# Linear-attention stage of a two-layer network: gate made by halves of an image, bias row added by GpSimd, first tokens turned later

## The chip, the cores and the metric

The kernel runs on one core of a Trainium2 chip, in fp32. The metric is the device time of one execution in microseconds (us), as the median of three runs: 2871.56 us before the change (2869.07 to 2872.76).

## What is computed

The input is 4 images of 32 x 32 pixels (1024 tokens) with 384 channels. Layer 0 is a deformable attention with convolved offsets; layer 1 is a linear attention and then a mixture of four experts of which each token takes two. Cut to what matters here:

```python
x = x + L0_conv(_gn(x), ...)          # ends in  out @ w_out + b_out
t = tokens(x)                          # 4 x 1024 tokens x 384
# layer 1, attention (12 heads of 32 channels)
q, k, v = split(_ln_t(t) @ qkv_w + qkv_b)
A = einsum('bhdn,bhne->bhde', f(k), f(v)) * gauss      # f(t) = t + 1 if t >= 0 else exp(t)
out = einsum('bhnd,bhde->bhne', q * d**-0.5, A - lam * A)
t = t + (out @ proj_w + proj_b)
# layer 1, experts
probs = softmax(_ln_t(t) @ gate_w + gate_b)            # 4 experts
masked = probs of the two largest, divided by their sum
h = gelu(_ln_t(t) @ w1[e] + b1[e]);  y = h @ w2[e] + b2[e]
t = t + sum over e of masked[e] * y[e]
```

`_ln_t` is a layer norm over the 384 channels.

## The kernel before

Tokens stand in tiles of 128 partitions by 384 channels, eight tiles an image. A token tile that goes into a matmul as the stationary or moving side has to be turned first (channels on partitions), by three 128x128 transposes on TensorE (PE) into PSUM and a copy to SBUF.[...]

**Layer 0 and its end (the first seam).** The work is cut into 24 units (image and head), each in `KP` = 4 steps, `NP` = 96 steps in all. A loop `for g in range(NP + 7)` (L1500 to L1559) issues the stages of a software pipeline by hand: in a manual schedule each engine gets its instructions in the order in which they are written. The last scores are done some steps before the last of these, so the last `g` hold only the tail of the pipeline: `values` (L1317, the product `po` of exponentiated scores S with v), `out_of` (L1348, ACT's copy `av`), `to_queries` (L1362, the turn `pr`, the reciprocal `ri` and the product `at`), `to_channels` (L1397, the turn `pi` and ACT's copy `ao`). When an image's six heads are through, `waiting` gets eight token tiles, and `project` (L1417) makes for each: load the input tile `xk` from memory, three matmuls `y`, GpSimd adds the bias row (L1438), DVE adds `y` (L1441), and the result is stored to `x1_d`. The tag `xk` has three places (bufs=3), which project's tiles rotate through. For the last image, the `while waiting` loop behind the main loop does these eight, with PSUM from three tags in turn.

In this tail the first layer norm of the linear stage is hidden: image 0's tokens, x0, have been loaded by `load_early`, and at `g == NP + 3` (L1549) all eight tiles are normalised by `layer_norm` (L1095: statistics of eight tiles, one inverse root, then tile by tile) into the tag `xk`, turned by PE (`c_tr`, L1555) and copied by ACT to `xT0`. In PE's written order these 24 transposes stand ahead of the last `po` product. The line `wqT` (L1725), nine transposes of a weight, is PE's first work of the linear stage.

**The linear stage.** It has no manual schedule; the order on each engine is that in which generators are stepped (L2020 to L2031):

```python
for part in (ahead, behind, behind):
    left = next(part, part) is not part or left
```

`ahead` is `keys(b + 1)` (L1907) and `behind` is `outputs(b)` (L1963), so the steps of two images alternate. `keys` normalises and turns the image's eight tiles, then makes for each tile keys and values (`c_kv`: six matmuls into two PSUM tiles), DVE's bias addition, the feature map (`ex`, Exp on ACT, then `fm` on DVE), and one tile later the product `pa`, 3 x 128 x 128; at its end `am` is `pa` times a constant mask. `outputs` folds `am` with the projection (`c_pg`, `c_g`), with the query weight (`c_pw`, `c_wx`) and the query bias (`c_pb`; with the projection's bias it is the row `rb`), each link waiting for the one before. Then come eight products `c_y` = turned tokens times `wx`. For each, DVE adds `rb` out of PSUM (`c_ysb`, L2011) and adds the sum to the token tile in xb (L2012). There is a step after every two tiles. PSUM: the tag `mm` has four banks, `tr` two, `ph` two.

At its end `outputs` steps through `gate(b)` (L1732): it stores the image's tokens to `out`, takes the layer norm's statistics of all eight tiles and one inverse root (`rstd_of`, L220: Sqrt on ACT and six small operations on DVE), then for each half of the image four times normalise (`tn`, L1747), turn (`d_tr`) and copy (`d_tT`), six matmuls `pl` for the logits, and a store of `tn` to memory (tn_d), where the experts gather tokens from. `tn` has one place, so the second half's first write waits for the first half's store. Then softmax and choice of two (small operations on DVE), the counts' products `pg` (L1810), the slots, 16 scatters of table entries by GpSimd (L1842), and the table of blocks. GpSimd takes its instructions in order, too: after image 0's round the call `fetch(0)` (L1659) puts a load of block 0's entries on SP's queue and a conversion and four gathers on GpSimd's.

**The experts (second seam).** 25 blocks of 512, 256 or 128 gathered tokens follow, each turned (`e_tr`), multiplied by w1 (`ph`, L2053) and w2 (`acc`, L2085). Block 0 needs image 0 only, but its turns stand in PE's order behind all of image 3's gate; with no image left to alternate with, nothing lies beside that gate.

Of the kernel before, what the change touches and what calls it, by code (L numbers as in the profile page):

```python
# [11 lines left out]
F32 = mybir.dt.float32  # L12
I32 = mybir.dt.int32
AF = mybir.ActivationFunctionType
ALU = mybir.AluOpType
# [4 lines left out]
P = 128  # L20
# [139 lines left out]
def body(  # L160
# [954 lines left out]
    with tc.tile_pool(name="b_w", bufs=1) as bwp, tc.tile_pool(name="b_qkv", bufs=2) as bq, tc.tile_pool(  # L1115
# [361 lines left out]

        with tc.manual_schedule(
# [22 lines left out]
            for g in range(NP + 7):  # L1501
# [47 lines left out]
                if g == NP + 3:  # L1549

                    for k, t in layer_norm(by, bm, x0, 0, "c_ln", tag="xk"):
                        if k % 4 == 0:
                            pt = bps.tile([P, 4, 512], F32, tag="s", name=f"c_tr0_{k}")
                        for c in range(CK):
                            nc.tensor.transpose(  # L1555
                                pt[:, k % 4, c * P : (c + 1) * P], t[:, c * P : (c + 1) * P], ident
                            )
                        nc.scalar.copy(
                            xT0[:, :, k * P : (k + 1) * P],  # L1559
                            pt[:, k % 4, :NC].rearrange("p (c j) -> p c j", c=CK),  # L1560
                        )
# [3 lines left out]
            while waiting:  # L1565
# [3 lines left out]
                for i in range(n):  # L1569
                    project(0, py[:, i, :])  # L1570
                    project(1)
                    project(2)

# [143 lines left out]
    with tc.tile_pool(name="c_1", bufs=1) as c1, tc.tile_pool(name="c_2", bufs=2) as c2, tc.tile_pool(  # L1717
# [14 lines left out]
        def gate(b):  # L1732

            nc.sync.dma_start(out_t[b].rearrange("(k p) c -> p k c", p=P), xb[b])
            mv = cs.tile([P, NB, 2], F32, tag="mv", name=f"d_lnmv{b}")
            for k in range(NB):
                st = cs.tile([P, 6], F32, tag="bn", name=f"d_lnbn{b}_{k}")
                nc.vector.bn_stats(st, xb[b][:, k, :])
                nc.vector.bn_aggr(mv[:, k, :], st)
            r = rstd_of(cs, mv[:, :, 1], 1e-5, [P, NB], f"d_lnr{b}")  # L1740

            pl = lmm.tile([P, 512], F32, tag="mm", name=f"pl{b}")
            for f in range(2):
                tT = c2.tile([P, CK, 512], F32, tag="tT", bufs=1, name=f"d_tT{b}_{f}")
                tn = c2.tile([P, 4, NC], F32, tag="tn", bufs=1, name=f"tn{b}_{f}")
                for k in range(4 * f, 4 * f + 4):
                    nc.vector.tensor_scalar(  # L1747
                        tn[:, k % 4, :], xb[b][:, k, :], mv[:, k, 0:1], r[:, k : k + 1], ALU.subtract, ALU.mult
# [158 lines left out]
        def keys(b):  # L1907
# [52 lines left out]
            am = c2.tile([P, CK, P], F32, tag="am", name=f"am{b}")  # L1960
# [4 lines left out]
        def outputs(b):  # L1965
# [31 lines left out]
            rb = c2.tile([P, NC], F32, tag="rb", name=f"c_rb{b}")  # L1997
            nc.vector.tensor_tensor(rb, ps[:, :NC], bproj, ALU.add)
            yield
# [206 lines left out]
```

## Time and profile before

| view | value |
|---|---|
| median of three runs | 2871.56 us |
| the profiled execution, its time beside its span | 2916.14 us, span 2914.4 us |
| PE busy, share of the span | 2620.1 us, 90% |
| DVE | 1589.4 us, 55% |
| ACT | 1149.0 us, 39% |
| GpSimd (POOL) | 817.4 us, 28% |
| mean granted PE clock | 0.959 |
| layer 0, to 1430 us: PE busy | 1199.1 of 1430.0 us |
| first seam, 1430 to 1480 us: PE busy | 36.1 of 50.0 us |
| linear stage to the first expert product, 1480 to 1814.6 us: PE busy | 303.2 of 334.6 us |
| experts, 1814.6 us to the end: PE busy | 1081.7 of 1099.8 us |
| DVE's two additions per y tile (L2011, L2012) | 32 x 0.543 and 32 x 0.558 us |
| GpSimd's addition of a row to a token tile (L1438) | 0.995 us |
| GpSimd's scatter of table entries (L1842) | 64 x 0.961 us |

The profile is of one execution, and all its times are from the start of its span. It is longer than the runs without a profiler, so sums made with its durations are compared with its own 2916.14 us first. A line such as L1555 is a line of the kernel. An instruction's idle time is that of its engine just before it, and the arrow names what ended that idle time; an engine named there as "remote" or "issue" is none that the profile could tell. A group or instruction that stands as "x3" in an order of time is three records that followed each other.

### The profile page before, as it was taken

To read this page: it belongs to the slowest core of one execution; us is meant where nothing else is said; L and a number is where in the kernel's file an instruction comes from. 1 tells how busy PE (TensorE), PEld (TensorE's weight loads), DVE (VectorE), ACT (ScalarE), POOL (GpSimd) and SP (SyncE) were. 2 spreads that over 40 slices of the span, in tenths; PEclk is the share of its full clock that TensorE was granted. 3 is DMA by queue.
4 is the path that set the end of the run, shared out by engine and by line. 5 is a ranking of instruction groups with operands and counts; after the bars stand their busy time and mean duration, and the time that the engine had idled before them with its cause. 6 is when DMAs were issued, how large, how long until landed. Compare 5 with 4: busy or idle time off the path is not lost. (4 is left out here: it accounts for less than half of the span.)

```text
span 2914.4 us, 33271 instructions
## 1 busy us (share of the span) xinstructions
PE 2620.1 (90%) x12731; PEld 1295.6 (44%) x12731; DVE 1589.4 (55%) x2357; ACT 1149.0 (39%) x1522; POOL 817.4 (28%) x744
## 2 busy tenths in 40 slices
PE   8679957888898988889799997999999999999999
PEld 5345522333333333233256554555555555555566
DVE  3668867999999999999647665101001101011011
ACT  4354526777767667666422221111111111111111
POOL 1528873232333323233000223322111112121121
PEclk9789977999999999999899998999999999999999
DMA  7824475554555655454121311543222334474271
GB/s 198 238 66 134 129 220 169 154 150 141 153 160 174 187 154 155 139 156 139 28 100 44 123 44 55 182 152 124 101 100 101 105 136 144 150 249 168 100 268 64
DMA packets 267899, 404.77 MB, mean 139 GB/s; under 512 B 134674, under 2 KB 207634, under 8 KB 267356
## 3 DMA queue, kind: packets, MB, share of 16 engines
q1 hardware_dynamic: 214912, 230.43, 25.1%
q0 software_dynamic: 52112, 172.15, 18.6%
q8 instruction: 100, 1.64, 0.2%
q14 instruction: 59, 0.48, 0.1%
q10 hardware_dynamic: 716, 0.07, 0.0%
HBM read 345.68 MB, written 70.06 MB: 143 GB/s over the span
## 5 line engine op out<-in xcount | busy, mean ns | idle before, releaser
L2053 PE MATMUL ph<-d_xT,w 128*128 128x512 f32 (+1 forms) x1152 | 483.9, 554 | 1.2 <-ACT h L2060 1.2
L2085 PE MATMUL acc<-w,h 128*128 128x384 f32 x1392 | 480.3, 486 | 0.0
L1221 PE MATMUL ps<-q,k 64*64 64x512 f32 x1536 | 384.0, 614 | 93.3 <-DVE S L1252 46.5
L1168 POOL DMA_INDIRECT win<-table,widx x192 | 279.7, 1457 | 643.0 <-DVE t L1194 611.7
L2060 ACT ACTIVATE h<-ph,b1c 128x512 f32<-128x512 f32 (+1 forms) x192 | 124.1, 647 | 776.3 <-PE ph L2053 711.5
L1226 PE MATMUL ps<-o,ident 64*64 64x512 f32 x1536 | 380.4, 615 | 8.4 <-ACT o L1202 8.4
L2085 PEld LDWEIGHTS acc<-w,h 128*128 128x128 f32 x1392 | 264.1, 190 | 208.5 <-issue 73.2
L2053 PEld LDWEIGHTS ph<-d_xT,w 128*128 128x128 f32 x1152 | 216.8, 191 | 196.2 <-issue 144.3
L871 POOL DMA_INDIRECT ga<-img,pidx x192 | 230.3, 1199 | 187.7 <-DVE w L828 65.7
L2115 POOL DMA_INDIRECT out<-rows,ei x67 | 67.2, 1002 | 700.0 <-DVE rows L2112 691.2
L1221 PEld LDWEIGHTS ps<-q,k 64*64 64x64 f32 x1536 | 99.2, 135 | 358.6 <-issue 215.4
L1315 ACT ACTIVATE S<-S 128x2048 f32<-128x2048 f32 x96 | 183.4, 1911 | 190.1 <-DVE S L1311 190.1
L1252 DVE SCALAR_TENSOR_TENSOR S<-t,bw,ps 128x1024 f32<-128x1024 f32 x192 | 236.9, 1275 | 21.0 <-PE ps L1226 18.0
L1194 DVE SCALAR_TENSOR_TENSOR t<-win,bw,t 128x1056 f32<-128x1056 f32 x192 | 244.5, 1314 | 5.2 <-ACT t L1184 4.0
L1709 DVE COPY d_xT<-e_tr 128x512 f32<-128x512 f32 (+2 forms) x75 | 36.5, 511 | 372.7 <-PE e_tr L1706 372.7
L2104 DVE SCALAR_TENSOR_TENSOR rows<-b2r,en,rows 128x384 f32<-128x384 f32 x67 | 40.8, 618 | 364.2 <-DMA rows<-out,ei 258.2
L1184 ACT ACTIVATE t<-win,bw 128x1056 f32<-128x1056 f32 x192 | 218.1, 1168 | 37.7 <-DMA win<-table,widx 36.4
L1202 ACT ACTIVATE o<-t,bw 128x1024 f32<-128x1024 f32 x192 | 212.8, 1144 | 37.2 <-DVE t L1194 29.2
L1311 DVE TENSOR_TENSOR S<-S,pbs 128x2048 f32<-128x2048 f32 x96 | 218.9, 2282 | 2.0 <-ACT pbs L1306 2.0
L1329 PE MATMUL po<-S,v 128*64 128x512 f32 x768 | 197.7, 638 | 23.8 <-ACT av L1354 13.6
L2112 DVE SCALAR_TENSOR_TENSOR rows<-acc,en,rows 128x384 f32<-128x384 f32 x67 | 41.4, 618 | 219.1 <-PE acc L2085 217.6
L713 PE MATMUL pcv<-qpad,wc 64*64 64x256 f32 x1728 | 121.4, 396 | 27.3 <-issue 26.6
(350 smaller groups left out, 3442.6 us busy)
## 6 DMA issues: line engine op xcount, KB each, us to landing
w<-in_L_ffn_w SPq DMA_DIRECT2D x50, 2304.0 KB
img<-in_x SPq DMA_DIRECT2D x48, 256.0 KB
q<-q_d SPq DMA_DIRECT2D x48, 256.0 KB
x<-in_x SPq DMA_DIRECT2D x8, 768.0 KB
q_d<-qt SPq DMA_DIRECT2D x24, 256.0 KB
v_d<-qkvw SPq DMA_DIRECT2D x32, 192.0 KB
v<-v_d SPq DMA_DIRECT2D x24, 256.0 KB
k<-k_d SPq DMA_DIRECT2D x48, 128.0 KB
```

Of the source, the lines that this page charges most:

```text
L871: nc.gpsimd.indirect_dma_start(out=ga[:, g].rearrange("p s c -> p (s c)"), out_offset=None, in_=img[b][:, :], in_offset=bass.IndirectOffse ...
L1168: nc.gpsimd.indirect_dma_start(out=win, out_offset=None, in_=tables[h // 2][:, :], in_offset=bass.IndirectOffsetOnAxis(ap=widx[b][:, nb, h ...
L1184: nc.scalar.activation(t.rearrange("p y x -> p (y x)"), wins[p, e][:, : HI * WIN], AF.Copy, scale=weight(p, e, 0),)
L1194: nc.vector.scalar_tensor_tensor(tf, wins.pop((p, e))[:, WIN:], weight(p, e, 1), tf, ALU.mult, ALU.add)
L1202: nc.scalar.activation(o, ts[p, e][:, :, 0:WI], AF.Copy, scale=weight(p, e, 2))
L1221: made.append(nc.tensor.matmul(ps[HALF[1 - r], e, FULL[f]], k[HALF[r], 2 * kp + e, :], q[HALF[r], FULL[f]], start=(step == 0), stop=(step ...
L1226: made.append(nc.tensor.matmul(ps[HALF[r], d, FULL[f]], ident[HALF[r], HALF[r]], os_[p, d][HALF[r], FULL[f]], start=(step == 0), stop=(ste ...
L1252: nc.vector.scalar_tensor_tensor(st[:, e, :].rearrange("p (y x) -> p y x", x=WI), ts.pop((p, e))[:, :, 1:WIN], weight(p, e, 3), ps[:, e, : ...
L1311: nc.vector.tensor_tensor(Ss[p], Ss[p], bc(pbss[p // KP][:, :], 1, 2), ALU.add)
L1329: nc.tensor.matmul(pos[i][0][HALF[f], :], vs[i][:, 2 * kp + e, :], Ss[p][:, e, FULL[f]], start=(first and e == 0), stop=(last and e == 1),)
L2053: nc.tensor.matmul(ph if short(d) else ph[:, :n], a, m, start=(c == 0), stop=(c == CK - 1))
L2085: nc.tensor.matmul(d["acc"][0 if short(d) else s][:, :NC], h[:, s * P : (s + 1) * P], d["w2"][:, hc, :], start=(hc == 0), stop=(hc == HC - 1),
```

## The change

- **First tokens turned later.** `layer_norm` of image 0 becomes a generator that the loop steps. At `g == NP + 3` it makes the statistics and the first normalised tile. `turn_first(n)` turns the tile at hand and normalises the next one: two tiles at `NP + 4`, two at `NP + 5`, one at `NP + 6`, one after each round of the `while waiting` loop, the rest at its end. The tag stays `xk` with three places, now shared with the projections of the last image.
- **Gate by halves.** Statistics and inverse root are made for four tiles at a time (`r` has four columns). The generator `gate(b)` is made before the y loop and stepped once after each of the tiles 4 to 7, so that a half's first tiles are turned beside the last y products. `tn` has two places. `am` and `rb` have one place in place of two.
- **Bias row by GpSimd.** After `rb`, GpSimd adds it to the image's eight token tiles in place; behind each y product one DVE addition adds `y` out of PSUM to the token tile. The tile `c_ysb` is gone.
- **Store of the tokens** to `out` moves from the start of the gate to behind the y loop, on SP's queue behind the first store of `tn`.

```diff
@@ -1473,6 +1473,26 @@
                     for i, k4 in enumerate(at):
                         values_copy(pl[:, i, :], k4)
                         values_store(b, f, k4)
+
+
+        first = layer_norm(by, bm, x0, 0, "c_ln", tag="xk")
+
+        def turn_first(n):
+            while n and state.get("first"):
+                k, t = state.pop("first")
+                if k % 4 == 0:
+                    state["pt"] = bps.tile([P, 4, 512], F32, tag="s", name=f"c_tr0_{k}")
+                pt = state["pt"]
+                for c in range(CK):
+                    nc.tensor.transpose(
+                        pt[:, k % 4, c * P : (c + 1) * P], t[:, c * P : (c + 1) * P], ident
+                    )
+                nc.scalar.copy(
+                    xT0[:, :, k * P : (k + 1) * P],
+                    pt[:, k % 4, :NC].rearrange("p (c j) -> p c j", c=CK),
+                )
+                state["first"] = next(first, None)
+                n -= 1
 
 
         with tc.manual_schedule(
@@ -1547,18 +1567,9 @@
                 if g == 15 * KP:
                     load_early()
                 if g == NP + 3:
-
-                    for k, t in layer_norm(by, bm, x0, 0, "c_ln", tag="xk"):
-                        if k % 4 == 0:
-                            pt = bps.tile([P, 4, 512], F32, tag="s", name=f"c_tr0_{k}")
-                        for c in range(CK):
-                            nc.tensor.transpose(
-                                pt[:, k % 4, c * P : (c + 1) * P], t[:, c * P : (c + 1) * P], ident
-                            )
-                        nc.scalar.copy(
-                            xT0[:, :, k * P : (k + 1) * P],
-                            pt[:, k % 4, :NC].rearrange("p (c j) -> p c j", c=CK),
-                        )
+                    state["first"] = next(first)
+                elif g > NP + 3:
+                    turn_first(2 if g < NP + 6 else 1)
 
             project(2)
             spots = [("x", 2), ("o0", 1), ("o1", 1)]
@@ -1570,6 +1581,8 @@
                     project(0, py[:, i, :])
                     project(1)
                     project(2)
+                turn_first(1)
+            turn_first(NB)
 
     ab_ctx.close()
     xpool = early_ctx.enter_context(tc.tile_pool(name="x", bufs=1))
@@ -1731,21 +1744,21 @@
 
         def gate(b):
 
-            nc.sync.dma_start(out_t[b].rearrange("(k p) c -> p k c", p=P), xb[b])
             mv = cs.tile([P, NB, 2], F32, tag="mv", name=f"d_lnmv{b}")
-            for k in range(NB):
-                st = cs.tile([P, 6], F32, tag="bn", name=f"d_lnbn{b}_{k}")
-                nc.vector.bn_stats(st, xb[b][:, k, :])
-                nc.vector.bn_aggr(mv[:, k, :], st)
-            r = rstd_of(cs, mv[:, :, 1], 1e-5, [P, NB], f"d_lnr{b}")
 
             pl = lmm.tile([P, 512], F32, tag="mm", name=f"pl{b}")
             for f in range(2):
+                half = slice(4 * f, 4 * f + 4)
+                for k in range(4 * f, 4 * f + 4):
+                    st = cs.tile([P, 6], F32, tag="bn", name=f"d_lnbn{b}_{k}")
+                    nc.vector.bn_stats(st, xb[b][:, k, :])
+                    nc.vector.bn_aggr(mv[:, k, :], st)
+                r = rstd_of(cs, mv[:, half, 1], 1e-5, [P, NB // 2], f"d_lnr{b}_{f}")
                 tT = c2.tile([P, CK, 512], F32, tag="tT", bufs=1, name=f"d_tT{b}_{f}")
-                tn = c2.tile([P, 4, NC], F32, tag="tn", bufs=1, name=f"tn{b}_{f}")
+                tn = c2.tile([P, 4, NC], F32, tag="tn", bufs=2, name=f"tn{b}_{f}")
                 for k in range(4 * f, 4 * f + 4):
                     nc.vector.tensor_scalar(
-                        tn[:, k % 4, :], xb[b][:, k, :], mv[:, k, 0:1], r[:, k : k + 1], ALU.subtract, ALU.mult
+                        tn[:, k % 4, :], xb[b][:, k, :], mv[:, k, 0:1], r[:, k % 4 : k % 4 + 1], ALU.subtract, ALU.mult
                     )
                     pt = ltr.tile([P, CK, P], F32, tag="tr", name=f"d_tr{b}_{k}")
                     for c in range(CK):
@@ -1957,7 +1970,7 @@
             product(*late.pop(0))
 
 
-            am = c2.tile([P, CK, P], F32, tag="am", name=f"am{b}")
+            am = c2.tile([P, CK, P], F32, tag="am", bufs=1, name=f"am{b}")
             nc.vector.tensor_tensor(am, pa, gm, ALU.mult)
             state[b] = xT, am
             yield
@@ -1994,8 +2007,11 @@
                     start=(c == 0),
                     stop=(c == CK - 1),
                 )
-            rb = c2.tile([P, NC], F32, tag="rb", name=f"c_rb{b}")
+            rb = c2.tile([P, NC], F32, tag="rb", bufs=1, name=f"c_rb{b}")
             nc.vector.tensor_tensor(rb, ps[:, :NC], bproj, ALU.add)
+            for k in range(NB):
+                nc.gpsimd.tensor_tensor(xb[b][:, k, :], xb[b][:, k, :], rb, ALU.add)
+            gates = gate(b)
             yield
             for k in range(NB):
                 ps = lmm.tile([P, 512], F32, tag="mm", name=f"c_y{b}_{k}")
@@ -2007,12 +2023,13 @@
                         start=(ci == 0),
                         stop=(ci == CK - 1),
                     )
-                y = c2.tile([P, NC], F32, tag="y", name=f"c_ysb{b}_{k}")
-                nc.vector.tensor_tensor(y, ps[:, :NC], rb, ALU.add)
-                nc.vector.tensor_tensor(xb[b][:, k, :], xb[b][:, k, :], y, ALU.add)
+                nc.vector.tensor_tensor(xb[b][:, k, :], ps[:, :NC], xb[b][:, k, :], ALU.add)
+                if k > 3:
+                    next(gates)
                 if k % 2:
                     yield
-            yield from gate(b)
+            nc.sync.dma_start(out_t[b].rearrange("(k p) c -> p k c", p=P), xb[b])
+            yield from gates
 
 
         for _ in keys(0):
```

## The prediction

> **What bounds the kernel now.** I first read busy time by stretch (columns: stretch, its length, PE, PEld, DVE, ACT, POOL busy with instruction counts, granted PE clock, DMA share, GB/s).
>
> ```profile
> 1430.00:1480.00 50.00, 36.13 (x126) 17.70 (x123) 16.46 (x76) 9.14 (x14) 8.87 (x20) 0.80 0.19 60
> 1530.00:1580.00 50.00, 50.00 (x200) 31.07 (x198) 37.92 (x94) 14.36 (x22) 0.00 (x0) 1.00 0.18 64
> 1780.00:1830.00 50.00, 33.44 (x116) 18.65 (x115) 31.38 (x140) 9.15 (x16) 13.59 (x16) 0.83 0.24 80
> 1880.00:1930.00 50.00, 50.00 (x138) 25.79 (x137) 4.85 (x8) 6.36 (x10) 11.84 (x13) 1.00 0.42 146
> ```
>
> PE bounds the linear stage and the experts. It has holes at both seams: before the linear stage (14 us of 50 idle) and between that stage and the experts (17 us). Only what shortens PE's holes counts. DVE's removed additions lie beside PE's work and are worth nothing by themselves.
>
> Then PE's instructions in order of time (start, duration, what; in brackets idle time before it and who ended it). The first seam:
>
> ```profile
> 1432.74 1.22 PE L1338 MATMUL po<-S,ones 128*32 128x512 f32 x8
> 1436.98 0.90 PE L1555 MATMUL c_tr<-ident,c_ln 128*128 128x128 f32 x3 [3.02 <-DVE c_ln L1105]
> 1448.10 2.95 PE L1329 MATMUL po<-S,v 128*64 128x512 f32 x8
> 1457.19 3.79 PE L1429 MATMUL y<-wo,ao 128*128 128x384 f32 x6 [1.20 <-ACT ao L1412]
> 1479.77 0.88 PE L1725 MATMUL wqT_tr<-ident,qkvw 128*128 128x128 f32 x6 [0.71 <-DVE xk L1441]
> ```
>
> The last attention product `po` stands 14 us behind eight transposes that need a layer norm. Everything after it starts late. The y phase, images 1 and 2, and the second seam:
>
> ```profile
> 1591.74 0.41 PE L1810 MATMUL pg<-cnt,tri 128*128 128x32 f32 x2 [1.04 <-DVE cnt L1798]
> 1622.88 9.70 PE L2003 MATMUL c_y<-c_wx,c_xT 128*128 128x384 f32 x24 [2.01 <-DVE c_ysb L2011]
> 1703.20 3.66 PE L1938 MATMUL c_kv<-qkvw,c_xT 128*128 128x384 f32 x6 [3.41 <-issue]
> 1814.60 3.62 PE L2053 MATMUL ph<-d_xT,w 128*128 128x512 f32 x4
> ```
>
> Last, GpSimd's and DVE's instructions in order of time. In image 1 GpSimd issues 16 scatters of table entries (one each 1.264 us), then waits for block 0's entries, converts them and issues four gathers; DVE waits for `y` and, at the second seam, for the store of `tn`:
>
> ```profile
> 1618.60 0.96 POOL L1842 DMA_INDIRECT tab_d<-ent,si  x1 [0.30 <-issue]
> 1624.70 0.61 POOL L1677 CAST ei<-en 128x8 int32<-128x8 f32 x1 [5.14 <-DMA en<-tab_d]
> 1629.40 0.95 POOL L1680 DMA_INDIRECT xr<-tn_d,ei  x1 [0.30 <-issue]
> 1702.59 0.56 DVE L2011 TENSOR_TENSOR c_ysb<-c_y,c_rb 128x384 f32<-128x384 f32 x1 [5.76 <-remote]
> 1781.12 0.56 DVE L2011 TENSOR_TENSOR c_ysb<-c_y,c_rb 128x384 f32<-128x384 f32 x1 [4.21 <-PE c_y L2003]
> 1801.10 1.65 DVE L1747 TENSOR_SCALAR tn<-xr,d_lnmv,d_lnr_r 128x384 f32<-128x384 f32 x4 [5.61 <-DMA tn_d<-tn]
> ```
>
> **Late hand-overs.** In images 1 to 3 DVE starts `c_ysb` up to 8.6 us after PE's records of that `y` end (1694.0 against 1702.59), always while the scatter runs or just after. Image 0, without a scatter, has none. I don't know the mechanism. It cost PE 2.6 us idle plus 1.8 of slow clock in image 1 (9.70 against 7.90 us for 24 matmuls) and 3.4 + 1.6 in image 2 (3.66 against 2.10), and DVE 4.2 us at the second seam.
>
> [...] 0.99 us (L1438) against 0.56 (L2012) for 128x384. [...] `c_kv` matmuls after the 3.41 us gap take 847 ns instead of 486.[...]
>
> **Part by part**, on the profiled run.
>
> *First tokens turned later.* Exp of the last scores ended at 1431.54, so `po` now follows at 1433.8 and ends at 1437.9 (2.95 + 1.06). On PE two turns of 1.47 us each (0.90 plus the wait for ACT's copy) come next; ACT copies `po` to av meanwhile (done by 1438.6), the turn back to queries, pr, takes 1.7, so it ends at 1442.0; the row's reciprocal and product on DVE take 1.0 while PE makes two more turns to 1444.4; the turn pi takes 1.1 and its copy ao on ACT 1.1: y starts at 1446.7, 10.5 us earlier. But the tag xk has three places. The turned token holds one until its transpose, so eight projections share two. One round of a place is store 1.87 + load 2.49 + GpSimd 0.99 + DVE 0.56 plus waits, some 6.4 us, 3.2 per tile; before it was 2.6 with three. The y phase was 22.6 us before (1457.19 to wqT at 1479.77). Followed tile by tile, with turns 5 to 7 between, the eight tiles now take 27.0 from 1446.7, so the last xk falls at 1473.7 instead of 1479.7. Gain 6.0, bounds 3 (queue worse) and 9.5 (no queueing).
>
> *pg.* The counts' products move behind two matmuls of `kv_6`; the 1.04 us wait in images 0, 1 and 2 goes: 3.1 (bounds 1.5, 3.1).
>
> *GpSimd's additions.* The 32 second DVE additions (32 x 0.56 = 17.9 us) go, 32 on GpSimd (31.7) come; both lie beside PE. Images 0, 2, 3: eight additions by 0.99 from rb on; y comes every 1.94 us, so they lead. In images 2 and 3 the scatter of the image before ends about when y_0 does; should it be late, PE still has four PSUM banks, 6 us. Image 1 is different. In the built order its additions stand on GpSimd behind the scatter (16 by 1.264 = 20.2 us) and block 0's fetch. The gate is now ready earlier: slots come about 1.0 after `kv_7_0` ends (call that K). Scatter to K+21; en, cast 6.0; four gathers 5.0: K+32; first addition K+33, DVE's K+33.6. PE's y_0 to y_3 fill the four banks by K+26.6. Behind DVE's waiting addition queue `kv_0` and everything else; PE's `kv_0_0` needs y_0's bank. PE idles 7.0, plus 1.7 slow clock: 8.7, against 4.5 lost there before: a loss of 4.2 (bounds 3 and 8.7, if an unprofiled run before has no late hand-over).
>
> *Gate by halves.* Eight more statistics groups of the small operations (6 by 0.2) and two more table loads per image (2.56 us) lie beside PE: ACT is 22 to 36% busy. Uncovered they'd be 3.8 us an image. At the second seam there is no cover and here is the gain. From y_0's start, T (1770.87): four y by 1.94 end y_3 at about T+8.0; its statistics, the root with its table load and four normalisations (0.47 each, among the other work of DVE) have the first half normalised by T+14.6, transposed among y_6, y_7. y_7's sum T+17.9, statistics T+18.65, rstd 1.5, first tn T+20.15, transposes T+20.7. Before they began at 1801.64 = T+30.8, since the second half waited 5.61 for the store of the single `tn`; from there to ph 12.96, unchanged. So ph at T+33.7 instead of T+43.7: 10.0. Of this 4.2 is the late hand-over that I assume stays: 5.8 counted (bounds 5 and 10). rb and am lose their second place: their last readers (GpSimd's additions, c_pg) are done some 40 us before the next writing, so nothing waits; if it did, PE would stand for one c_pb, 2 us. On ACT the first root waits for DVE's y_3 with ex_0 queued behind it; fm_0 is read one kv round (4.5 us) later, which covers it. out's store moves behind tn's first store on SP, seven us later in the queue, read by nobody before ph.
>
> *Sum*: -6.0 - 3.1 + 4.2 - 5.8 = -10.7. The experts move whole (PE 967.5 of 980 busy). Profiled execution 2916.1, expected 2905.4. Its median unprofiled is 44.6 lower; the same difference off 2871.6 gives 2860.9.
>
> **Rivals.** *Hand-overs on time*: the scatter now ends before y, so image 2's 5.0 and the seam's 4.2 go too: -19.9, 2851.7. For: image 0. Against: the moved scatter covers other hand-overs. Chance 0.20. *GpSimd eats it*: the hand-overs are the profiler's, image 1 costs 8.7 and the tail gives 3 to 6: -6.0 - 3.1 + 8.7 - 5.8 = -6.2 down to -1.7, around 2867.5. Image 0's smooth y speaks for it; 0.24. *Slower*: the scatter, ten us earlier, falls on c_pg, c_g, c_pw, c_wx, where each hand-over stalls PE at once. With 2.7 and 8.6 late and 1.7 slow clock, 13.0 in three images is 39.0 in place of 13.7: +25.3, less the 14.9 of the tail, pg and the seam: +10.4, 2882. It decides from 7.8 us of lateness an image (3 x (7.8 + 1.7) = 28.5, against 13.7 + 14.9 = 28.6). Against: c_pw of image 3 ran under a scatter unharmed. 0.05. The forecast: 0.51.
>
> **Numbers.** 2860.9; range 2851 to 2870, from the second case to GpSimd's worst; forecast alone 2857 to 2866. A measurement of this kernel tells 0.2% (5.7 us) from no change. Faster: the forecast, the second and a little of the third, 0.72; same 0.23; slower 0.05.
>
> **Signs.** Right: po directly behind po at 1434, y at 1447, wqT near 1474; in image 1 DVE waits for POOL at the first addition, some 10 us, PE 7; no DMA wait before the last four tn; y_0 of image 3 to ph 34 to 38 us. Wrong: a later wqT, waits for GpSimd in images 2 and 3, or PE idle in c_pg to c_wx beyond 3 us an image.

## The result

Measured: 2854.49 us median of 16 runs (2848.20 to 2865.70), against 2869.66 us of the kernel before in as many runs (2859.25 to 2874.74). The ratio is 0.9947, 95% interval 0.9937 to 0.9956: 15.2 us or 0.5% faster. The forecast was 2860.9 us, 10.7 us faster, with a range of 2851 to 2870 and 2857 to 2866 for the likeliest case alone.

The profiled execution of the changed kernel has a span of 2846.1 us, and its time, 2848.20 us, is the lowest of the 16. The first profile of before, on which the prediction was built, has 2914.4. That gap of 68 us is not the change: an unchanged kernel before was profiled again (the first experiment below) and has 2868.1. Comparisons of stages are made with that second profile where not said otherwise.

**Stages.** I took five points out of the order of PE's and ACT's instructions in each trace: the end of the last exp of scores (ACT, S), the first `wqT`, the first `c_y` of each image, the first `ph`, and the end of the span. All figures are the time from one point to the next, in us.

| kernel | last exp to wqT | wqT to y of image 0 | image 0 to 1 | 1 to 2 | 2 to 3 | y of image 3 to ph | ph to end |
|---|---|---|---|---|---|---|---|
| before, first profile | 48.2 | 52.5 | 75.0 | 81.8 | 81.8 | 43.7 | 1099.8 |
| before, second profile | 50.7 | 52.4 | 75.1 | 82.0 | 76.1 | 37.7 | 1099.1 |
| changed | 37.4 | 52.1 | 75.2 | 84.8 | 76.3 | 32.3 | 1097.5 |

So nearly all of it comes from the first seam (-13.3) and the second (-5.4); image 1 gives 2.8 back. Together with the other stages the table has -17.4 from the last exp on, and the medians of the runs say -15.2; the profiled execution of the changed kernel was its fastest.

**The changed kernel's lines.** Busy time by stretch, first seam, linear stage and second seam, each 50 us long and set to the same events as before:

```profile
1389.00:1439.00 50.00, 41.45 (x169) 22.80 (x166) 23.38 (x91) 12.80 (x20) 8.85 (x20) 0.94 0.42 137
1479.50:1529.50 50.00, 50.00 (x207) 30.87 (x206) 36.94 (x103) 16.92 (x25) 7.68 (x8) 1.00 0.18 64
1725.50:1775.50 50.00, 41.85 (x145) 21.92 (x145) 30.04 (x160) 10.45 (x19) 19.34 (x21) 0.93 0.25 81
```

At the first seam PE is busy for 41.5 us at a granted clock of 0.94; the two profiles of before have 36.1 us at 0.80 and 36.6 at 0.74. At the second seam it is 41.9 us at 0.93, where before has 33.4 at 0.83 and 39.0 at 0.90. The middle stretch was full before and still is.

PE in order of time, the first seam:

```profile
1388.26 3.44 PE L1329 MATMUL po<-S,v 128*64 128x512 f32 x8 [2.30 <-ACT S L1315]
1392.63 1.94 PE L1329 MATMUL po<-S,v 128*64 128x512 f32 x8
1395.84 0.55 PE L1487 MATMUL c_tr<-ident,c_ln 128*128 128x128 f32 x3 [0.28 <-DVE c_ln L1105]
1402.31 2.20 PE L1429 MATMUL y<-wo,ao 128*128 128x384 f32 x6 [1.20 <-ACT ao L1412]
1421.18 3.38 PE L1429 MATMUL y_x<-wo,ao 128*128 128x384 f32 x6 [2.91 <-DVE xk L1441]
1427.81 0.85 PE L1738 MATMUL wqT_tr<-ident,qkvw 128*128 128x128 f32 x6 [0.80 <-DVE xk L1441]
```

The last exp ended at 1390.4. The last `po` (at 1392.63) now stands directly behind the `po` before it, and a turn takes 0.55 us where it took 0.90. The y phase still waits for `xk` (2.91).

The linear stage and the second seam:

```profile
1530.09 0.32 PE L1823 MATMUL pg<-cnt,tri 128*128 128x32 f32 x2
1540.93 0.52 PE L1926 MATMUL c_tr<-ident,c_ln 128*128 128x128 f32 x3 [1.77 <-DVE c_ln L1105]
1570.78 6.54 PE L1951 MATMUL c_kv<-qkvw,xT 128*128 128x384 f32 x12 [7.37 <-DVE xr L2026]
1648.04 4.03 PE L1951 MATMUL c_kv<-qkvw,c_xT 128*128 128x384 f32 x12
1702.01 1.65 PE L1937 MATMUL pa<-fm 128*128 128x128 f32 x6 [2.93 <-DVE fm L1965]
1736.68 0.91 PE L1765 MATMUL d_tr<-ident,tn 128*128 128x128 f32 x6 [1.22 <-DVE tn L1760]
1748.56 3.62 PE L2070 MATMUL ph<-d_xT,w 128*128 128x512 f32 x4
```

`pg` has no wait in front of it any more, but `c_tr` and `pa` have new ones. In image 1 PE stands idle for 7.37 us. In image 2 it does not wait at the place where the first profile of before had 3.41. The second half of the last gate waits 1.22 where DVE had waited 5.61 for a store.

GpSimd and DVE in image 1:

```profile
1557.65 0.96 POOL L1855 DMA_INDIRECT tab_d<-ent,si  x1 [0.30 <-issue]
1563.49 0.19 POOL L1690 CAST ei<-en 128x8 int32<-128x8 f32 x1 [4.89 <-PE c_y L2019]
1568.16 0.95 POOL L1693 DMA_INDIRECT xr<-tn_d,ei  x1 [0.30 <-issue]
1569.13 7.66 POOL L2013 TENSOR_TENSOR xr<-xr,c_rb 128x384 f32<-128x384 f32 x8
1570.17 0.56 DVE L2026 TENSOR_TENSOR xr<-c_y,xr 128x384 f32<-128x384 f32 x1 [14.52 <-POOL xr L2013]
```

Scatter, entries, gathers, then the eight additions: DVE has been idle for 14.52 us when it first takes a `y` of image 1. It waits for the additions of images 2 and 3 as well, 4.62 and 1.95 us, and there PE loses nothing.

### The profile page after: what moved, and what is told of

The parts are those of the page before. It is cut to its first block, busy times and chain, and to the rows that moved or that the text cites. A ratio compares the mean times of both kernels' runs of the same rounds, so it can differ in the third digit from the quotient of the medians.

```text
span 2846.1 us, 33342 instructions
## 1 busy us (share of the span) xinstructions
PE 2586.8 (91%) x12731; PEld 1283.8 (45%) x12731; DVE 1579.4 (55%) x2349; ACT 1157.8 (41%) x1532; POOL 855.1 (30%) x776
## 3 DMA queue, kind: packets, MB, share of 16 engines
q1 hardware_dynamic: 214912, 230.43, 25.6%
## 5 line engine op out<-in xcount | busy, mean ns | idle before, releaser
L1722 DVE COPY d_xT<-e_tr 128x512 f32<-128x512 f32 (+2 forms) x75 | 36.6, 512 | 386.1 <-PE e_tr L1719 386.1
L2121 DVE SCALAR_TENSOR_TENSOR rows<-b2r,en,rows 128x384 f32<-128x384 f32 x67 | 40.9, 618 | 359.9 <-DMA rows<-out,ei 321.1
L1270 DVE TENSOR_TENSOR m<-m,S 128x2048 f32<-128x2048 f32 x48 | 117.1, 2440 | 1.6
```

## The experiments

The twelve runs were made in three groups. The last two groups ran on two other chips, on which the kernel before took 2941 and 2947 us. Layer 0 is some 60 us longer there: the last exp ends at 1450 to 1471 us in their profiles, and at 1390 to 1396 in those of the result and of the first group. Ratios are against before in the same group, and are compared with each other only within a group.

### Before, profiled again

No edit.

> The kernel before, unchanged, for a second profile, since the first profiled execution lay 44 us over the median of the others. My theory (the stage lengths of the first profile hold, only layer 0 was longer): wqT to the first expert product 334 to 335 us again, last exp of scores to wqT 48 us, span near 2868 with the 44 us taken from layer 0. Rival (the first profile's seams were long because its clock was low): last exp to wqT 44 to 46 us, and wqT to ph 325 to 330. Rival (late hand-overs are an accident of that one execution): images 1 and 2 show no PE idle time in the y phase, wqT to ph 320 to 325.

Measured: 2869.81 us, span 2868.1; 50.7 us from last exp to wqT, 323.3 from wqT to ph. My theory failed for the stages, and the third expectation came true: this execution has no late hand-overs. Whether that goes by the execution or by the chip is taken up at the end. Of the 46.3 us between the two spans, 36.6 lie in layer 0 and 11.5 in the linear stage; the first seam is 2.5 longer here. The first seam on PE:

```profile
1400.40 0.90 PE L1555 MATMUL c_tr<-ident,c_ln 128*128 128x128 f32 x3 [3.14 <-DVE c_ln L1105]
1422.72 4.12 PE L1429 MATMUL y<-wo,ao 128*128 128x384 f32 x6 [1.20 <-ACT ao L1412]
1445.71 0.55 PE L1725 MATMUL wqT_tr<-ident,qkvw 128*128 128x128 f32 x3 [0.70 <-DVE xk L1441]
```

The exp ended at 1395.0: y starts 27.8 us behind it (25.6 in the first profile), and eight turns run at 0.90 us. In image 1, in the middle of the scatter (which starts at 1565.52), DVE takes `y` every 1.94 us, so nothing is late. But a wait stands where the first profile had none to speak of (0.81). DVE, PE, and two stretches of busy time:

```profile
1578.23 0.56 DVE L2011 TENSOR_TENSOR c_ysb<-c_y,c_rb 128x384 f32<-128x384 f32 x1
1614.34 1.65 DVE L1747 TENSOR_SCALAR tn<-xr,d_lnmv,d_lnr_r 128x384 f32<-128x384 f32 x4 [4.78 <-DMA tn_d<-tn]
```

```profile
1614.97 0.87 PE L1752 MATMUL d_tr<-ident,tn 128*128 128x128 f32 x3 [4.51 <-DVE tn L1747]
```

```profile
1600.00:1605.00 5.00, 5.00 (x24) 3.12 (x23) 5.00 (x15) 2.59 (x5) 0.00 (x0) 1.00 1.06 372
1605.00:1615.00 10.00, 5.49 (x34) 3.46 (x32) 4.12 (x12) 5.00 (x7) 0.00 (x0) 0.97 0.81 295
```

The second half's `tn` waits for the first half's store. On SP's queue that store stands behind the loads of block 0's weights (2 x 2304 KB) and the store of the tokens to `out` (1536 KB), and the DMA share is 1.06 and 0.81 in these stretches. In image 2's round, which has no such load, DVE waits only 0.42 us at this place. I had found this wait only at the second seam.

### First tokens turned later, alone

```diff
+        first = layer_norm(by, bm, x0, 0, "c_ln", tag="xk")
...
                 if g == NP + 3:
-                    for k, t in layer_norm(by, bm, x0, 0, "c_ln", tag="xk"):
...
+                    state["first"] = next(first)
+                elif g > NP + 3:
+                    turn_first(2 if g < NP + 6 else 1)
```

> Only the first tokens turned later; gate and additions as before. My theory: po follows po directly, and last exp to wqT is some 40 us against 48: 6 to 8.6 us faster, ratio 0.9970 to 0.9979; the linear stage is 334 us as before. Rival (the eight projections with two places set the pace, so that the tail gives little): 0 to 3 us, ratio 0.999 to 1. Rival (the gain is lost to a colder PE in the linear stage): tail 8 us shorter and the linear stage longer by as much.

Measured: 2856.92 us against 2871.61, ratio 0.9946 (0.9933 to 0.9959): 11.8 to 19.2 us faster. Last exp to wqT is 38.2 us against 50.7, the linear stage 322.3 against 323.3. The direction of my theory held, its size did not: I had 48 to some 40 us. The gain is twice what I allowed, and part of that is the base of 48. Nothing is given back later, so the third expectation falls; and the second one falls too. The first `y` starts 11.9 us behind the exp (which ended at 1394.2), as in the changed kernel:

```profile
1406.11 2.20 PE L1429 MATMUL y<-wo,ao 128*128 128x384 f32 x6 [1.20 <-ACT ao L1412]
```

### Gate by halves, alone

```diff
-                y = c2.tile([P, NC], F32, tag="y", name=f"c_ysb{b}_{k}")
-                nc.vector.tensor_tensor(y, ps[:, :NC], rb, ALU.add)
-                nc.vector.tensor_tensor(xb[b][:, k, :], xb[b][:, k, :], y, ALU.add)
+                nc.vector.tensor_tensor(ps[:, :NC], ps[:, :NC], rb, ALU.add)
+                nc.vector.tensor_tensor(xb[b][:, k, :], ps[:, :NC], xb[b][:, k, :], ALU.add)
+                if k > 3:
+                    next(gates)
...
```

The gate, its halves, the numbers of places and the later store of the tokens are those of the changed kernel; GpSimd adds nothing.

> Only the gate by halves with two places for tn, the later store, and one place for am and rb; both additions stay on DVE (the first writes back into PSUM, so that no c_ysb tile is needed). My theory: the pg waits go (3.1), the seam from image 3's first y to ph is 32 to 34 us against 43.7 (10), and the scatter now ends when y begins, so the late hand-overs of images 1 and 2 go too (up to 9.5): 13 to 22 us faster, ratio 0.9923 to 0.9955. Rival (late hand-overs exist only under the profiler): 9 us faster, ratio 0.997. Rival (the earlier scatter makes hand-overs of c_pg to c_wx late, which cost as much): no faster, ratio 1.

Measured: 2857.14 us, ratio 0.9954 (0.9942 to 0.9966): 13.2 us by the ratio. Image 1 to 2 is 74.8 us in place of 82.0, the second seam 32.7 in place of 37.7, image 0 to 1 74.7. So it is in the range, but with other parts than I gave: there were no late hand-overs to lose. Most of image 1's 7.2 us is the wait for the store of `tn`, which is gone: 4.51 us, and some 1.4 of slower matmuls right behind it (in the second profile of before, three `d_tr` take 0.87 and twelve `c_kv` 5.09 us there, and 0.49 and 4.04 a little later). The rest I can't place. The `pg` waits of images 0 to 2 went, and PE waits for `c_ln` and `fm` instead, in image 0's round:

```profile
1560.19 0.52 PE L1913 MATMUL c_tr<-ident,c_ln 128*128 128x128 f32 x3 [1.77 <-DVE c_ln L1105]
```

### Bias row by GpSimd, alone

```diff
+            for k in range(NB):
+                nc.gpsimd.tensor_tensor(xb[b][:, k, :], xb[b][:, k, :], rb, ALU.add)
...
-                y = c2.tile([P, NC], F32, tag="y", name=f"c_ysb{b}_{k}")
-                nc.vector.tensor_tensor(y, ps[:, :NC], rb, ALU.add)
-                nc.vector.tensor_tensor(xb[b][:, k, :], xb[b][:, k, :], y, ALU.add)
+                nc.vector.tensor_tensor(xb[b][:, k, :], ps[:, :NC], xb[b][:, k, :], ALU.add)
```

> Only the additions by GpSimd, the gate as before. My theory: the scatter still runs into the y phase, so the additions start late: in image 1 behind the scatter and block 0's fetch (about 16 us of PE idle in place of 2.6), in image 2 behind the scatter (5 to 7 in place of 3.4), at the second seam 3 later; 12 to 20 us slower, ratio 1.004 to 1.007. Rival (DVE's freed 18 us were what held the y phase, GpSimd leads anyway): same or up to 5 us faster. Rival (late hand-overs do the harm and not GpSimd's queue): within 3 us of before.

Measured: 2889.52 us, ratio 1.0063 (1.0050 to 1.0076): 18 us slower, as my theory had it in sum. By place it was different: 82.6, 85.1 and 46.5 us in images 1, 2 and the seam against 82.0, 76.1 and 37.7. GpSimd and PE in image 1, and PE in image 2:

```profile
1587.48 0.96 POOL L1842 DMA_INDIRECT tab_d<-ent,si  x1 [0.30 <-issue]
1588.46 7.67 POOL L2000 TENSOR_TENSOR xr<-xr,c_rb 128x384 f32<-128x384 f32 x8
1596.08 0.18 POOL L1677 CAST ei<-en 128x8 int32<-128x8 f32 x1
```

```profile
1590.12 5.83 PE L1938 MATMUL c_kv<-qkvw,xT 128*128 128x384 f32 x12 [5.12 <-DVE xr L2012]
```

```profile
1672.91 7.20 PE L1938 MATMUL c_kv<-qkvw,c_xT 128*128 128x384 f32 x12 [5.47 <-DVE xr L2012]
```

In this build the additions stand between scatter and fetch, so PE stands 5.12 us in image 1 and not 16. The stage is only 0.6 longer for it, since the wait for the store of `tn` (PE 4.51) is gone there. Image 2, which has no fetch in it, loses as much to the scatter alone, and its stage is 9.0 longer. With the old gate the scatter ends in the middle of the y phase; with halves it ends as y begins.

### Image 1's additions on DVE

```diff
-                nc.gpsimd.tensor_tensor(xb[b][:, k, :], xb[b][:, k, :], rb, ALU.add)
+                (nc.vector if b == 1 else nc.gpsimd).tensor_tensor(
+                    xb[b][:, k, :], xb[b][:, k, :], rb, ALU.add
+                )
```

> The changed kernel, with image 1's eight bias additions on DVE and those of the other images on GpSimd. My theory (the loss of the change is image 1's additions standing behind the scatter and block 0's fetch on GpSimd: 84.8 us from y_0 of image 1 to y_0 of image 2, where the gate alone had 74.8): PE's 7.4 us gap is gone, 75 us, some 10 us faster than the changed kernel, ratio 0.990 to 0.992. Rival (DVE's 4.5 us ahead of y_0 take the place of the wait): gap of 2 to 4 us, ratio 0.992 to 0.993. Rival (the additions wait for something else, the scatter itself): no change, 0.9947.

Measured: 2897.05 us against 2941.44, ratio 0.9863 (0.9820 to 0.9906). Image 1 to 2 is 74.6 us, as with the gate alone, and wqT to ph 310.5 against 320.8; a changed kernel with GpSimd's additions, profiled on this same chip (it is the one with room for the first tokens, below), has 84.7 for image 1 to 2. PE's gap of 7.37 us is gone and the other stages stay:

```profile
1628.43 4.03 PE L1951 MATMUL c_kv<-qkvw,xT 128*128 128x384 f32 x12
```

That is my theory by the stages. The ratio can't be set beside the 0.9947 of another chip.

### All additions on DVE

```diff
-                nc.gpsimd.tensor_tensor(xb[b][:, k, :], xb[b][:, k, :], rb, ALU.add)
+                nc.vector.tensor_tensor(xb[b][:, k, :], xb[b][:, k, :], rb, ALU.add)
```

> The changed kernel, with all 32 bias additions on DVE ahead of y, none on GpSimd. My theory (work taken off DVE is worth nothing, since PE bounds the stage; GpSimd's part of the change is a pure loss): as fast as with image 1 alone on DVE, ratio 0.990 to 0.992. Rival (in images 0, 2, 3 GpSimd's help is real and DVE's 4.5 us ahead of y_0 delay the gate): 2 to 6 us slower than with image 1 alone, 0.992 to 0.994.

Measured: 2904.80 us, ratio 0.9868 (0.9825 to 0.9910), beside 0.9863 on the same chip: the times can't tell the two apart. wqT to ph is 312.4 against 310.5, of which 1.5 lie at the second seam (34.2 against 32.7), where DVE has no cover. So the 24 additions of the other three images are worth 0 to 2 us on GpSimd, most of it at the seam, and the eight of image 1 cost 10.

### Two places for tn, twice

```diff
-                tn = c2.tile([P, 4, NC], F32, tag="tn", bufs=1, name=f"tn{b}_{f}")
+                tn = c2.tile([P, 4, NC], F32, tag="tn", bufs=2, name=f"tn{b}_{f}")
...
-                y = c2.tile([P, NC], F32, tag="y", name=f"c_ysb{b}_{k}")
-                nc.vector.tensor_tensor(y, ps[:, :NC], rb, ALU.add)
-                nc.vector.tensor_tensor(xb[b][:, k, :], xb[b][:, k, :], y, ALU.add)
+                nc.vector.tensor_tensor(ps[:, :NC], ps[:, :NC], rb, ALU.add)
+                nc.vector.tensor_tensor(xb[b][:, k, :], ps[:, :NC], xb[b][:, k, :], ALU.add)
```

`am` and `rb` have one place, too. The same kernel ran in the second and in the third group.

> The kernel before with two places for tn, one for am and rb, and the first addition written back into PSUM (which frees the room); the gate stays whole. My theory (image 1's tn waits for its store behind block 0's weights: 4.5 us of PE idle and 1.7 of slow clock): 75 to 76 us from y_0 of image 1 to y_0 of image 2 in place of 82.0, the second seam 37.2 in place of 37.7; 6 to 7.5 us faster, ratio 0.9974 to 0.998. The rest of what the gate by halves gave is then the halves. Rival (the halves do it all, since they start the store earlier): within 2 us of before. Rival (the places do it all): ratio 0.9955.

> The kernel before with two places for tn and the first addition in PSUM once more, since the first such run had late hand-overs in images 1 to 3 that hid what the places do. My theory: where no hand-over is late, y_0 of image 1 to y_0 of image 2 is 75 to 76 us in place of 82.0, the seam 37 us, ratio 0.9974 to 0.998. Rival (halves and not places took away image 1's wait): 82, ratio 0.999 to 1.001. Where hand-overs are late again, both images 1 and 2 stand at 81 to 83.

Measured: 2943.74 us, ratio 1.0016 (0.9995 to 1.0037), and 2942.68 us, ratio 0.9991 (0.9965 to 1.0016). Image 1 to 2 is 81.4 and 82.4 us. DVE in image 2 of the first of them, then PE:

```profile
1719.29 0.57 DVE L2010 TENSOR_TENSOR c_y<-c_y,c_rb 128x384 f32<-128x384 f32 x1 [5.67 <-issue]
1727.73 0.57 DVE L2010 TENSOR_TENSOR c_y<-c_y,c_rb 128x384 f32<-128x384 f32 x1 [6.46 <-remote]
```

```profile
1728.94 4.21 PE L1938 MATMUL c_kv<-qkvw,c_xT 128*128 128x384 f32 x6 [5.62 <-DVE xr L2011]
```

The late hand-overs of the first profile are there again in images 1 to 3, in both runs, and cover what the places do. At the seam (47.6 and 47.7 us) four operations of block 0's output rows stood in DVE's order within the gate as well (`pg` waited 8.60 in place of 3.59). In neither run does a `tn` wait for a store, at the seam neither, where DVE had waited 5.61 and 3.98 us in the two profiles of before: two places alone end that wait there. Neither run tells whether the places, the halves or the later store of the tokens took away image 1's 7.2 us; that stays open, and the store was not moved alone.

### Room of their own for the first tokens

```diff
-            t = pool.tile([P, NC], F32, tag=tag, name=f"{name}{b}_{k}")
+            if pool is None:
+                t = own[:, k * NC : (k + 1) * NC]
+            else:
+                t = pool.tile([P, NC], F32, tag=tag, name=f"{name}{b}_{k}")
```

`own` is the tile `ao` of an earlier image, which has been read by then.

> The changed kernel, with room of their own for image 0's eight normalised tokens (the place of an earlier image's attention outputs), so that the projections have all three places of xk. My theory (the eight projections are paced by the rounds of xk's places): from the first of these y to wqT 22 to 23 us in place of 25.5, 2 to 4 us faster than the changed kernel, ratio 0.9932 to 0.994. Rival (the load and store latencies of each round pace it whatever the places): as the changed kernel, 0.9947. Rival (PE's own work paces it): as the changed kernel too, with PE busy throughout.

Measured: 2916.61 us, ratio 0.9914 (0.9879 to 0.9949). From the first of these y to wqT it takes 22.7 us against 25.5, and last exp to wqT 34.6 against 37.4. PE in order of time:

```profile
1484.43 2.20 PE L1433 MATMUL y_x<-wo,ao 128*128 128x384 f32 x6 [0.72 <-DVE xk L1445]
1494.53 2.20 PE L1433 MATMUL y_x<-wo,ao 128*128 128x384 f32 x6 [1.10 <-DVE xk L1445]
```

The wait for `xk` is 1.10 where it was 2.91: by stages my theory holds, with 2.8 us. The three profiles with this room have 20.9 to 22.7 us from the first of these `y` to `wqT`, the five with the shared places 25.5 to 26.3. The times alone would not show it.

### Both repairs, and the changed kernel beside it

Image 1's additions on DVE and room for the first tokens, the two diffs above together.

> The changed kernel with two repairs: image 1's bias additions on DVE, and room of their own for image 0's normalised tokens. My theory (the two losses are apart, 10 us and 3 us): wqT to ph 310 to 311 us in place of 320.8, exp to wqT 34.5 in place of 37.4; against the changed kernel 12 to 14 us faster, against before 27 us, ratio 0.990 to 0.991 where before has no late hand-overs. Rival (what is gained in the tail is given back, since the linear stage then waits for something that ends at a fixed time, such as loads): 8 to 10 us faster than the changed kernel.

> The changed kernel again, on the chip of this call, to compare the others with. My theory: exp to wqT 37.4, wqT to ph 321, ratio about 0.9947 where before has no late hand-overs, 0.991 where it has. Rival (its lead depends on the chip by more than the late hand-overs): stage lengths other than these by over 3 us.

Measured on one chip: 2906.22 us, ratio 0.9860 (0.9816 to 0.9904), and 2918.64 us, ratio 0.9900 (0.9870 to 0.9931) for the changed kernel. Last exp to ph is 33.1 + 311.6 = 344.7 us against 38.0 + 321.1 = 359.1, 14.4 us less; the medians are 12.4 apart, but the intervals of the two ratios overlap. The two losses are apart from each other, as my theory had it. The changed kernel's stages are those of its first profile to within 1 us (image 1 to 2: 85.6 against 84.8). From the last exp to ph the kernel with both repairs is the shortest of those that were run.

The changed kernel is 28 us faster than before on this chip, and 15 us in the result, on the other. Why is not shown, since the kernel before was not profiled here. Its near relative with two places for `tn` was: last exp to ph is 391.9 us there, against 359.1, and it has the late hand-overs of the first profile in three images. So they are a likely part of it.

### The block table made later

```diff
+            if b == B - 1:
+                table(b)
+
+        def table(b):
...
+                rounds += 1
+                if b and rounds == 2:
+                    table(b - 1)
+                    if b == 1:
+                        first = fetch(0, dw0, ds0)
```

On top of the two repairs.

> As the kernel with the two repairs, but the block table of images 0 to 2 (some 30 small DVE operations) is made in the next image's round, behind the first normalised tiles, and block 0's fetch follows it. My theory (the pg waits that the gate by halves took away came back as waits for c_ln and fm, because slots and table then stand ahead of these on DVE): the waits of 1.77 + 0.54, 1.46 + 0.54 and 2.93 + 0.65 us with slow clock behind shrink to about half, 3 to 6 us faster than with the two repairs. Rival (the slots' operations and the wait for kv_7 set c_ln's time, not the table): within 1.5 us of it. Rival (a later table makes block 0's entries late): ph later by 2 us or more.

Measured: 2927.16 us, ratio 0.9946 (0.9924 to 0.9967): some 21 us slower than with the two repairs, 84.8 and 85.3 us in place of 75.6 and 75.5 in the first two images. PE, then ACT, in image 1:

```profile
1606.33 0.52 PE L1933 MATMUL c_tr<-ident,c_ln 128*128 128x128 f32 x3 [1.09 <-DVE c_ln L1109]
1615.91 0.91 PE L1998 MATMUL c_pw<-c_g,wqT 128*128 128x384 f32 x2 [2.24 <-issue]
1618.77 1.61 PE L1998 MATMUL c_pw<-c_g,wqT 128*128 128x384 f32 x2 [1.95 <-issue]
1622.33 6.42 PE L1998 MATMUL c_pw<-c_g,wqT 128*128 128x384 f32 x14 [1.95 <-issue]
```

```profile
1618.24 0.48 ACT L1992 COPY c_g<-c_pg 128x384 f32<-128x384 f32 x1 [2.39 <-issue]
1621.80 0.48 ACT L1992 COPY c_g<-c_pg 128x384 f32<-128x384 f32 x1 [3.08 <-issue]
```

The wait for `c_ln` fell from 1.78 to 1.09 us, and in the next image from 1.46 to 0.77: the table's operations ahead of it on DVE make part of it, as my theory had it. But the forecast missed: hand-overs between PE and ACT became late under the scatter, on `c_pg` to `c_pw`. That is the mechanism of the prediction's slower rival, in a kernel other than the changed one.

## Why the prediction was right

The direction, the range and the likeliest case's sign held; three of its terms did not, and the measured time lies 2.5 us below the narrower range of that case.

- **Tail, -6.0 predicted, -13.3 shown.** The mechanism is as said: `po` follows the exp after 2.2 us where I had 2.3. The term was mis-sized in three places that add up to 7.3. The last `po` and the "two turns of 1.47 us each" were priced from rows in which PE ran at a low clock (granted 0.50 from 1437 to 1448 us, 0.73 from 1448 to 1452), so that y was put 15.2 us behind the exp. In the changed kernel that stretch runs at a granted 1.00: the last `po` ends 5.2 us behind the exp in place of 6.4, a turn takes 0.55, and y starts at 11.9 (3.3). "The eight tiles now take 27.0" was 25.5 (1.5). And the 48.2 us of before were a short sample: four other profiles with the old tail and its gate or additions changed have 51.3, 54.3, 48.7 and 54.6, the repeated before 50.7 (2.5).
- **pg, -3.1 predicted, nothing shown.** Its waits went, but image 0 to 1 stayed at 75.1 to 75.2. Slots and table, ready earlier, now stand on DVE ahead of `c_ln` and `fm`: PE waits 1.77 + 0.54 us there, and 2.93 in the last round. The later table took 0.7 of the wait for `c_ln` away, so the table is part of the cause; the rest is not shown. I asked who waits for `pg` and not what its followers on DVE would stand in front of.
- **Image 1, +4.2 predicted, +2.8 shown, by other parts.** GpSimd's queue is as said: PE idle 7.37 for 7.0, slow clock 6.54 - 4.04 = 2.5 for 1.7, together 9.9 for 8.7. The granted clock is 0.63 over these 6.54 us of twelve `c_kv` and 1.00 where twelve take 4.04; in the first profile of before it is 0.82 over the 9.70 us and 0.59 over the 3.66 us that the prediction calls slow. That it costs 10 is shown by image 1's additions on DVE (84.7 and 84.8 to 74.6). What it was set against was wrong: not 4.5 us of late hand-overs but 7.2 us, most of it the wait for the store of `tn`. The first profile had 1.08 us of that wait on DVE, and its late hand-overs had given the store time; that this is the reason is argued, not shown.
- **Second seam, -5.8 predicted, -5.4 shown.** From image 3's y to ph it takes 32.3 us; the step said 33.7, and 37.9 with the late hand-over that was assumed to stay. That assumption did not hold, and neither did the base: the second profile of before has 37.7 and not 43.7. The two errors cancel in the difference, which is luck. A table load on ACT takes 1.28 us in the first profile of before and in the changed kernel's, as in the 2.56 of the sum for two.
- **The base.** "Its median unprofiled is 44.6 lower; the same difference" was a step without ground. The second profiled execution of before (2869.81) stands at the median of the others (2871.61): so the profiler adds nothing that shows here, and the first profile was of an execution with a longer layer 0 (36.6 us) and late hand-overs. As a difference the step did no harm; as a reading of that trace it put the late hand-overs of three images into the sum.
- **The rivals.** That `y` is handed over on time was true in the profiles of the result, of before as well, so it was worth nothing here. The case in which GpSimd eats the gain had its price right (8.7 for 9.9) and the tail too small.
- **The signs.** PE idle of 7 in image 1 came true (7.37), and so did the end of the waits for a store before `tn`. DVE's wait was 14.52 and not some 10, and 32.3 from image 3's y to ph lies below the 34 to 38 given. One sign of being wrong came true without harm: DVE waits for GpSimd in images 2 and 3 (4.62 and 1.95 us).
- **GpSimd beside DVE.** The sum charged nothing for a GpSimd addition and one of the new DVE additions at the same time. In the first profile of before, DVE's additions of the projections (L1441, `y` out of PSUM) take 556 to 558 ns, beside one of GpSimd's (1466.72 us, GpSimd's from 1465.96 to 1466.95) or alone. In the changed kernel's it is the same: the 16 DVE additions that overlap one of GpSimd's take 537 to 559 ns, the 16 others 551 to 558. GpSimd's own 32 take 983 to 1004 ns, for the 0.99 us of the sum.

Two mistakes of opposite sign met: the tail gave 7.3 more, `pg` 3.1 less. With image 1 and the seam it comes to -10.7 - 7.3 + 3.1 - 1.4 + 0.4 = -15.9, against -15.2 measured; -1.6 from ph to the end is left out of this sum. The range did not need the two to meet: with the error of the tail alone the forecast would have been 2853.6, with that of `pg` alone 2864.0, and both lie in it. That it came as near as 4.5 us to the difference is in part luck.

## What to carry to other kernels

Price work that moves into a stretch where TensorE is busy with that stretch's clock, not with that of the gap it comes from: a turn of 0.90 us at a granted clock of 0.50 became one of 0.55 at 1.00. A sum of a few microseconds needs a second profile of the same kernel, since two executions can differ: in image 1 DVE waited 1.08 us for a store in the first profile of before and 4.78 in the second, and late hand-overs stood in the first alone. And work that is handed to a less busy engine stands in that engine's order: 24 of the 32 additions were worth 0 to 2 us on GpSimd, and the other eight, behind a scatter and a fetch, cost 10.

## What the runs showed of the hardware

Late hand-overs while GpSimd issues a scatter come and go with one and the same program: they are in the first profile of before and not in the second. The changed kernel's two profiles, from two chips, differ in this way as well. In the first one DVE takes the product `c_pb` of image 3 as soon as PE's records of it end, in the second one it starts 2.67 us later, though it was idle (PE, then DVE, first profile; then the second):

```profile
1714.35 2.10 PE L2003 MATMUL c_pb<-c_g,bqs 128*128 128x384 f32 x6
1716.49 0.56 DVE L2011 TENSOR_TENSOR c_rb<-c_pb,bproj 128x384 f32<-128x384 f32 x1 [11.83 <-PE c_pb L2003]
```

```profile
1775.06 2.10 PE L2003 MATMUL c_pb<-c_g,bqs 128*128 128x384 f32 x6
1779.83 0.56 DVE L2011 TENSOR_TENSOR c_rb<-c_pb,bproj 128x384 f32<-128x384 f32 x1 [14.26 <-PE c_y L2019]
```

One thing seems to go with them. In the scatter of the kernel with both repairs one issue is long, in that with the later table none is (GpSimd in image 1, one line from each):

```profile
1607.41 2.53 POOL L1859 DMA_INDIRECT tab_d<-ent,si  x1 [0.30 <-DVE c_ln L1109]
```

```profile
1607.01 0.96 POOL L1859 DMA_INDIRECT tab_d<-ent,si  x1 [0.30 <-DVE r_ind L1908]
```

The 14 profiles hold 42 scatters of images 0 to 2. In 26 of them one of the first ten issues takes over 1.2 us (1.3 to 2.5), and behind none of these does PE stand idle for a late hand-over in the y phase. Of the 16 without one, 11 are followed by late hand-overs (three each in the first profile of before and in both runs with two places for tn, two with the later table), two are not, and in three, those of the additions alone, DVE waits for GpSimd in any case and it can't be told.

But a long issue does not keep hand-overs on time. In six of the 26, all in image 3's round and in kernels with the changed gate on the two other chips, DVE starts `c_rb` 1.6 to 2.7 us after PE's records of `c_pb` end. With all additions on DVE it takes the first `y` of images 1 and 2 after 1.54 and 2.09 us of idle time, though PE's records of that `y` end before DVE becomes idle. PE goes on with further `y` at once in these cases. Two of them have a wait of PE for `tn` at the seam that may come of it (0.67 us with the later table, 1.49 with all additions on DVE, beside the 1.2 that all have). So a long issue is no sign that hand-overs are on time. The chip goes with the lateness more closely: `c_rb` is late in all six profiles with the changed gate on the two other chips, and in neither of the two from the result and the first group. Both profiles with the old gate and two places for `tn` on those chips have late `y`, and those of before and of the first tokens alone in the first group have none. Chip and kernel were not varied apart from each other, save for the changed kernel, and the cause stays open.
